# A change of buffer layout, of one scaling's engine and of six relu blocks' places at the seams of a two-layer graph kernel

## The chip, the cores and the metric

The kernel runs on one core of one Trainium2 chip, in float32 throughout. The metric is the device time of one execution in microseconds (us). The kernel before the change takes 2812.73 us, the median of three runs (2812.05 to 2813.75). Its profile is of one execution of 2812.97 us, whose recorded span is 2811.2 us.

A core has five engines with a queue each, which work through their own instructions in the order in which they were written down and wait for each other through semaphores: TensorE (PE; PEld is its loading of weights), VectorE (DVE), ScalarE (ACT), GpSimd (POOL) and SyncE (SP), which only starts transfers here. Matmuls write to PSUM; all other data lie in SBUF.

## The reference

There are 128 graphs of 64 tokens with 768 features. The input is normalised per token and cut at zero; two layers of attention over the given adjacency follow, and the input is added at the end:

```python
for l in range(2):
    m_left = einsum('bsh,oh->bso', h, W_left[l])
    m_right = einsum('bsh,oh->bso', h, W_right[l])
    u_left = einsum('bih,bjh->bij', h, m_left) / sqrt(768)
    u_right = einsum('bih,bjh->bij', h, m_right) / sqrt(768)
    u = u_left * adj_tri + u_left * diag_mask + u_right * swapaxes(adj_tri, 1, 2)
    e = exp(u) * adj
    attention = e / (sum(e, axis=2) + 1e-10)
    h_lin = einsum('bsh,oh->bso', h, W_lin[l]) + b_lin[l]
    ctx = matmul(attention, h_lin)
    h = relu(layer_norm(ctx, ln_a[l], ln_b[l]))
return x + h
```

## The kernel before, in words

**Passes.** The work is done in four passes, one after the other: `pass_one(0)`, `pass_two(0)`, `pass_one(1)`, `pass_two(1)` (L683 to L686). A pass goes over 16 blocks `u` of 512 tokens. Pass one of a layer projects a block with the left and the right weights (`project`, L344) and makes the attention from it (`scores`, L370, with a chain of small steps called softmax); the attention goes to DRAM. Pass two makes `h_lin` (`linear`, L607), multiplies the attention with it (`context`, L541) and normalises (`finish`, L566). In layer 0 the normalised rows `z` go to DRAM, four stores for each pair of row blocks (L594); the first pass of layer 1 loads them again as `x` (`load_rows`, L226, L243), transposes them on DVE to `xb` (L314), stores these (L310), loads them back feature by feature as `ht` (L248) and applies relu with `ln_a` and `ln_b` on ACT (`affine`, L250, L255), six instructions of 128x512 for a block.

**Matrix products.** A 768 by 768 product is done in 15 products of thirds of the features, with sums of weights and of tokens made ahead (a fast matrix multiplication). `ORDER` (L109) gives them: step 0 goes to PSUM bank X, 1 to Z, 2 to X, 3 to Y, and so on. The sums of tokens `ts` are made on POOL (L144; eleven for a block, 13 buffers). `read` (L182) brings a bank into the outputs, `m` in pass one and `hl` in pass two: the first product of an output is copied by ACT (L189), the others are added by DVE (L144). A bank is not written again before it has been read: step 2 stands still until ACT has read X of step 0.

**Order.** Nothing is scheduled by a tool. Each step runs two numbered slots (`run(base + 2 * i)` after its first half and `run(base + 2 * i + 1)` after its reads), and `put` and `put_all(slot, fs, step)` enter what else is to be issued in each slot, on whichever engine. So a slot settles the place of an instruction among the others of its engine. In the last block of pass two the two halves of the rows are done one after the other (L661, L663), 30 slots each, and the first block of the next layer is made ready beside them: `load_h(1, 1, 0)`, the six relu instructions from slot 22 and the sums of tokens from slot 30 (L658 to L660).

**End of the pass.** After the last half, `finish(u, 1)` (L666) runs the last context and normalisation: two squares on ACT (L577) with their sums, a square root (L579), the inverse on DVE (L582, L583), and for each of two row blocks a scaling (`scaled`, L585; on ACT in layer 0, L592) and its two stores.

**Buffers.** Each pass opens a pool of its own, and the pool of the next pass takes the same bytes of SBUF. Inside a pool the names get their places in the order in which they are first asked for. The pools are opened with `reuse_waits="tile"`: the first write of a tile waits for the last use of those old tiles that lay on its bytes, and for no others. By the built program, in KB from the start of the pool (`hl` is two buffers, `at` three, `x` and `adj` two, `z` three):

| pool | places before the change |
|---|---|
| pass one, layer 0 | `x` 0-12, `adj` 12-16, `xb` 16-28, `m` 28-52, `wm` 52-54 |
| pass two, layer 0 | `at` 0-3, `hl` 3-27, `z` 27-36, `x` 36-48, `xb` 48-60 |
| pass one, layer 1 | `adj` 0-4, `x` 4-16, `xb` 16-28, `m` 28-52, `wm` 52-54 |
| pass two, layer 1 | `a`, `b` 0-6, `at` 6-9, `hl` 9-33, `z` 33-45, `xr` 45-57 |

`wm` and `adj` are worked on by the softmax of the last block until the end of pass one (L396 to L414), after PE has gone on to pass two.

Of the kernel before, what the change touches and what calls it, by code (L numbers as in the profile page):

```python
# [10 lines left out]
F32 = mybir.dt.float32  # L11
I32 = mybir.dt.int32
AF = mybir.ActivationFunctionType
# [4 lines left out]
def kernel(  # L18
# [24 lines left out]
    nc = tc.nc  # L43
    B, S, H = x.shape
    L = w_lin.shape[0]
    P = 128
    C = H // P
# [4 lines left out]
    Q = 4  # L52
    T = Q * P
    TH = T // 2
    NB = B * S // T
# [203 lines left out]
    def transpose_rows(l, u, pool):  # L259
# [57 lines left out]
        todo.append(store)  # L317
        return todo


    def pass_one(l, aside):
        with tc.tile_pool(name=f"one{l}", bufs=2, reuse_waits="tile") as sp:
            ADJ, CHAIN, M = {}, {}, {}

            def load_adj(u):
                ADJ[u] = sp.tile([P, Q, 2, S], F32, name="adj")
# [200 lines left out]
    def pass_two(l, aside):  # L527
        last = l == L - 1
        with tc.tile_pool(name=f"two{l}", bufs=2, reuse_waits="tile") as sp:
            if last:  # L530
                for name, src in (("a", ln_a), ("b", ln_b)):
                    row(name, src[l], 0, H, sp.tile([P, H], F32, name=name, bufs=1))
            AT, HL = {}, {}

            def load(u):
                if (2, l, u) not in HT:
                    load_h(2, l, u)
                AT[u] = sp.tile([P, Q, S], F32, name="at", bufs=3)
                nc.sync.dma_start(AT[u], ATT[l][u])

            def context(u, r):  # L541


                hl, at = HL[u], AT[u]
                lo, hi = slice(0, S), slice(S, P)
                cx = [ps_aux.tile([P, 2, T], F32, name="aux") for _ in range(2)]
                for n in range(2):
                    for (j, k, i) in ((lo, 0, lo), (hi, 0, hi), (lo, 1, hi), (hi, 1, lo)):
                        q = r + 2 * k
                        m = n if j == lo else 1 - n  # L550
                        nc.tensor.matmul(cx[k][i, m, :HH], at[j, q, :], hl[j, q, m * HH:(m + 1) * HH],  # L551
                                         start=True, stop=True)
                return [c[:, :, :HH] for c in cx]

            def batch(r, k, h):
                return 4 * (h if k == 0 else 1 - h) + r + 2 * k

            XS = {}

            def residual(u, r):  # L560
                XS[u, r] = [sp.tile([P, H], F32, name="xr", bufs=4) for _ in range(2)]
                for k in range(2):
                    for h in range(PAIR):
                        nc.sync.dma_start(XS[u, r][k][h * S:(h + 1) * S], x[u * NBB + batch(r, k, h)])

            def finish(u, r):  # L566

                cx = context(u, r)
                zs = [sp.tile([P, H], F32, name="z", bufs=4 if last else 3) for _ in range(2)]
                if last and not u and not r:  # L570
                    residual(u, r)
                two = "p (n d) -> p n d"
                ss = stat.tile([P, 2], F32, name="ss")
                sd = stat.tile([P, 2], F32, name="sd1")
                rs = stat.tile([P, 2], F32, name="rs1")
                for k in range(2):
                    nc.scalar.activation(zs[k].rearrange(two, n=2), cx[k], AF.Square, accum_out=ss[:, k:k + 1])  # L577

                nc.scalar.activation(sd, ss, AF.Sqrt, bias=floor, scale=1.0 / (H - 1.0))  # L579

                def inverse():
                    nc.vector.tensor_scalar_add(rs, sd, EPS_LN)  # L582
                    nc.vector.reciprocal(rs, rs)  # L583

                def scaled(k):  # L585
                    if last:
                        nc.vector.scalar_tensor_tensor(  # L587
                            zs[k].rearrange(two, n=2), cx[k], rs[:, k:k + 1],
                            rows["a"].rearrange(two, n=2), op0=ALU.mult, op1=ALU.mult)
                        nc.gpsimd.tensor_add(zs[k], zs[k], rows["b"])  # L590
                        return
                    nc.scalar.activation(zs[k].rearrange(two, n=2), cx[k], AF.Copy, scale=rs[:, k:k + 1])  # L592
                    for h in range(PAIR):
                        nc.sync.dma_start(ROWS[u][batch(r, k, h)], zs[k][h * S:(h + 1) * S])  # L594

                def done(k):
                    if last:
                        xs = XS[u, r]
                        nc.vector.scalar_tensor_tensor(xs[k], zs[k], 0.0, xs[k], op0=ALU.max, op1=ALU.add)
                        for h in range(PAIR):  # L600
                            nc.sync.dma_start(out[u * NBB + batch(r, k, h)], xs[k][h * S:(h + 1) * S])
                        if k and (u < NB - 1 or r == 0):
                            residual(u + r, 1 - r)

                return [inverse] + [lambda k=k: scaled(k) for k in range(2)] + [lambda k=k: done(k) for k in range(2)]

            def linear(u, rs, base, ends, more):  # L607

                b, w = tokens_of((2, l, u)), W[l, "n"]
                if rs[0] == 0:  # L610
                    HL[u] = sp.tile([P, Q, H], F32, name="hl", bufs=2)
                hl, seen = HL[u], set()
                bank = {"X": AHEAD.pop()}
                early = {0: 3, 2: 5, 6: 9}
                for i, (s, at, t, _) in enumerate(ORDER):
                    if i in FIRST and i not in PRELOAD:
                        bank[at] = fresh(l, i, rs)
                    p = bank[at]
                    for n, r in enumerate(rs):
                        for c in range(K2):  # L620
                            nc.tensor.matmul(p[:, n], b[t][:, c, r * P:(r + 1) * P], w[s][:, c, :],  # L621
                                             start=(i in FIRST and i not in PRELOAD and n == c == 0),
                                             stop=(c == K2 - 1), skip_group_check=True)
                        if n == 0:
                            run(base + 2 * i)
                    read(p, lambda o: hl[:, o % 2 * 2 + rs[0]:o % 2 * 2 + rs[0] + len(rs), o // 2 * D:(o // 2 + 1) * D],
                         i, seen)
                    if i in early:
                        bank[FIRST[early[i]][0]] = fresh(l, early[i], rs)
                    if i == 11 and more:  # L630
                        AHEAD.append(fresh(l, 0, more))
                    if i in ends:
                        what, slots = ends[i]
                        for f, n in zip(finish(*what), slots):
                            put(n, f)
                    run(base + 2 * i + 1)

            load(0)
            for u in range(NB):
                turn = not last and u >= NB - 2  # L640
                if u + 1 < NB:
                    load(u + 1)
                    put_all(9 if u else 15, affine(2, l, u + 1))
                    put_sums_t((2, l, u + 1), 15 if u else 21, 1, 0)
                    if turn:
                        load_rows(1, 0, sp)
                        put_all(10, transpose_rows(1, 0, sp), 2)
                    if u in aside:
                        aside[u]()
                    ends = {}  # L650
                    if u:
                        ends = {0: ((u - 1, 0), (6, 7, 8, 11, 12)), 7: ((u - 1, 1), (20, 21, 22, 30, 30))}
                    linear(u, (0, 1), 0, ends, (0, 1) if u + 2 < NB else (0,))
                    for n in sorted(plan):
                        plan[n - 30] = plan.pop(n)
                else:
                    if turn:
                        load_h(1, 1, 0)  # L658
                        put_all(22, affine(1, 1, 0))
                        put_sums_t((1, 1, 0), 30, 2, 30)  # L660
                    linear(u, (0,), 0, {0: ((u - 1, 0), (12, 13, 15, 19, 21)),  # L661
                                        11: ((u - 1, 1), (34, 35, 36, 42, 44))}, (1,))
                    linear(u, (1,), 30, {4: ((u, 0), (50, 51, 52, 56, 58))}, ())  # L663
                    for n in sorted(plan):
                        run(n)
                    for f in finish(u, 1):  # L666
                        f()
# [48 lines left out]
```

## Time and profile before

| what | us |
|---|---|
| time, median of three | 2812.73 |
| span of the profiled execution | 2811.2 |
| pass one, layer 0, with the start | 0 to 936 |
| pass two, layer 0 | 936 to 1412 |
| pass one, layer 1 | 1412 to 2323 |
| pass two, layer 1 | 2323 to 2811 |
| step of 8 matmuls at full pace | 1.73 |
| step of 4 matmuls (last block of pass two, by halves) | 0.86 |

The ends of the passes are where the timeline shows the first matmul of the next one. A line of the timeline or of the groups names the source line, the engine, the operation, what it writes and reads, and in square brackets how long its engine stood idle ahead of it and what ended that. A line of the waits gives who waited for whom, then the sum in us, the number of times, and the longest.

### The profile page before, as it was taken

What the parts mean: (1) busy time and instruction counts of PE and PEld (TensorE: products, weight loads), DVE (VectorE), ACT (ScalarE), POOL (GpSimd) and SP (SyncE); (2) the same over time, 40 slices, a digit from 0 to 9 for tenths busy, and PEclk for the clock granted to TensorE, in tenths of its full rate; (3) what the DMA queues carried; (4) which work ended last, traced back from release to release, by engine and by line L of the source; (5) the groups of instructions that cost most, each with busy time, mean ns of one, the idle gap of its engine ahead of it and who ended that gap; (6) DMA issues with size and microseconds to landing.
All of it is one profiled execution on the core that took longest, in us unless ns stands there. A gap on an engine that the chain in (4) does not pass through costs nothing.

```text
span 2811.2 us, 46104 instructions
## 1 busy us (share of the span) xinstructions
PE 2755.9 (98%) x18712; PEld 2343.6 (83%) x18712; DVE 1338.1 (48%) x2222; ACT 838.0 (30%) x1453; POOL 1189.7 (42%) x935
## 2 busy tenths in 40 slices
PE   7999999999999999999999999999999999999997
PEld 6888888888888888888778888888888888888885
DVE  6455554454444332322334434443444335666666
ACT  2122222322231244444422121112111214545443
POOL 3343333223323455565423343223322335887875
PEclk9999999999999999999999999999999999999999
DMA  5632443234322243333563432343234304555654
GB/s 156 165 76 74 100 116 78 74 96 120 79 73 76 98 159 110 99 125 105 148 159 84 119 92 74 83 117 94 74 80 118 75 25 145 159 170 160 184 161 124
DMA packets 234068, 310.80 MB, mean 111 GB/s; under 512 B 54144, under 2 KB 184448, under 8 KB 225664
## 3 DMA queue, kind: packets, MB, share of 16 engines
q1 hardware_dynamic: 233568, 307.06, 39.9%
q8 instruction: 149, 2.44, 0.4%
q10 hardware_dynamic: 288, 0.79, 0.1%
q14 instruction: 63, 0.52, 0.1%
HBM read 202.91 MB, written 104.86 MB: 109 GB/s over the span
## 4 chain that ended last, share of the span: by engine, by line
PE 94%; DVE 2%; issue 1%; DMA 1%; POOL 1%; ACT 1%; SPq 0%; DVEq 0%; ACTq 0%; POOLq 0%
PE X L356 23%; PE V L356 15%; PE X L621 12%; PE Y L356 11%; PE Z L356 8%; PE V L621 8%; PE Y L621 6%; PE aux L382 5%; PE Z L621 4%; PE aux L551 3%; POOL w_r L144 1%; DVE m L144 0%; DMA z<-z 0%; DVE wm L396 0%; DMA x<-in_x_dram 0%
## 5 line engine op out<-in xcount | busy, mean ns | idle before, releaser
L144 POOL TENSOR_TENSOR ts<-ht 128x512 f32<-128x512 f32 x441 | 585.5, 1339 | 1249.1 <-DMA ht<-h 560.8
L189 ACT ACTIVATE m<-X 128x512 f32<-128x512 f32 x256 | 152.3, 595 | 1117.8 <-PE X L356 585.9
L144 POOL TENSOR_TENSOR ts<-ht,ts 128x512 f32<-128x512 f32 x189 | 248.8, 1324 | 155.4 <-PE X L621 78.2
L144 DVE TENSOR_TENSOR m<-m,V 128x512 f32<-128x512 f32 x256 | 174.2, 681 | 272.0 <-PE V L356 272.0
L144 DVE TENSOR_TENSOR m<-m,X 128x512 f32<-128x512 f32 x256 | 163.8, 681 | 252.0 <-PE X L356 251.4
L356 PE MATMUL X<-ts,w_l 128*128 128x256 f32 x1024 | 246.6, 384 | 10.7 <-ACT m L189 5.1
L621 PE MATMUL X<-w_n,ts 128*128 128x256 f32 x1024 | 245.1, 381 | 6.0 <-ACT hl L189 5.7
L356 PE MATMUL X<-ts,w_r 128*128 128x256 f32 x1024 | 241.9, 379 | 0.0
L144 DVE TENSOR_TENSOR m<-m,Z 128x512 f32<-128x512 f32 x128 | 88.0, 688 | 322.7 <-ACT m L189 254.4
L356 PEld LDWEIGHTS X<-ts,w_l 128*128 128x128 f32 x1024 | 194.1, 192 | 43.0 <-issue 6.0
L621 PEld LDWEIGHTS X<-w_n,ts 128*128 128x128 f32 x1024 | 192.0, 190 | 37.6 <-ACT hl L189 6.3
L356 PEld LDWEIGHTS X<-ts,w_r 128*128 128x128 f32 x1024 | 192.3, 190 | 28.7
L255 ACT ACTIVATE ht<-ht,b_col,a_col 128x512 f32<-128x512 f32 x192 | 143.1, 804 | 149.2 <-DMA ht<-h 149.2
L621 PE MATMUL Y<-w_n,ts 128*128 128x256 f32 x768 | 182.9, 380 | 0.0
L356 PE MATMUL Y<-ts,w_l 128*128 128x256 f32 x768 | 181.8, 380 | 0.0
L356 PE MATMUL Y<-ts,w_r 128*128 128x256 f32 x768 | 181.4, 379 | 0.0
L189 ACT ACTIVATE hl<-X 128x512 f32<-128x512 f32 (+1 forms) x136 | 77.7, 571 | 332.8 <-PE X L621 323.2
L621 PEld LDWEIGHTS Y<-w_n,ts 128*128 128x128 f32 x768 | 146.5, 191 | 20.1
L356 PEld LDWEIGHTS Y<-ts,w_l 128*128 128x128 f32 x768 | 146.4, 191 | 20.1
L356 PEld LDWEIGHTS Y<-ts,w_r 128*128 128x128 f32 x768 | 145.9, 190 | 19.8
L590 POOL TENSOR_TENSOR z<-z,b 128x768 f32<-128x768 f32 x64 | 115.4, 1814 | 95.4 <-DVE z L587 95.4
L144 DVE TENSOR_TENSOR hl<-hl,X 128x512 f32<-128x512 f32 (+1 forms) x136 | 83.2, 653 | 146.2 <-PE X L621 144.3
(105 smaller groups left out, 4680.7 us busy)
## 6 DMA issues: line engine op xcount, KB each, us to landing
ht<-h SPq DMA_DIRECT2D x63, 1536.0 KB, 7.2
h<-xb SPq DMA_DIRECT2D x124, 384.0 KB, 6.5
z<-z SPq DMA_DIRECT2D x128, 192.0 KB, 2.8
x<-z SPq DMA_DIRECT2D x128, 192.0 KB, 8.6
xr<-in_x_dram SPq DMA_DIRECT2D x128, 192.0 KB, 3.8
out_dram<-xr SPq DMA_DIRECT2D x128, 192.0 KB, 2.6
x<-in_x_dram SPq DMA_DIRECT2D x120, 192.0 KB, 8.5
adj<-in_adj_dram SPq DMA_DIRECT2D x64, 128.0 KB, 2.7
```

The source lines that it names most:

```text
L144: (eng.tensor_add if sign == "+" else eng.tensor_sub)(o, a, b)
L189: nc.scalar.activation(to(o), p, AF.Copy, scale=1.0 if sign == "+" else -1.0)
L255: nc.scalar.activation(ht, ht, AF.Relu, bias=cols[1][:, c:c + 1], scale=cols[0][:, c:c + 1])
L356: nc.tensor.matmul(p[:, g], w[ORDER[i][0]][:, c, g * P:(g + 1) * P], b()[t][:, c, :], start=(new and g == c == 0), stop=(c == K2 - 1), ski ...
L382: nc.tensor.matmul(p[h * S + e:h * S + e + 32, q, e:e + 96], ht[:, c, b * S + e:b * S + e + 32], mb[:, e:e + 96], start=(c == 0), stop=(c ...
L551: nc.tensor.matmul(cx[k][i, m, :HH], at[j, q, :], hl[j, q, m * HH:(m + 1) * HH], start=True, stop=True)
L590: nc.gpsimd.tensor_add(zs[k], zs[k], rows["b"])
L621: nc.tensor.matmul(p[:, n], b[t][:, c, r * P:(r + 1) * P], w[s][:, c, :], start=(i in FIRST and i not in PRELOAD and n == c == 0), stop=(c ...
```

## The change

It has three parts.

- **Layout.** A new helper `places` asks once for a tile of each name at the start of a pool, in a chosen order, and does nothing with it; with that the names' places are settled. In pass one of layer 0 the order becomes `x`, `xb`, `m`, `adj`, `wm`; in pass two of layer 0 `hl`, `at`, `x`, `xb`, `z`; in pass one of layer 1 `m`, `adj`, `x`, `xb`, `wm`. Pass two of layer 1 is left as it is. The aim is that a tile which is written first in a pass lies on tiles that the pass ahead has long been done with.
- **The last scaling on two engines.** In the last block's last `finish` of layer 0 the second of the two scalings goes to DVE.
- **The first relu blocks of the next layer spread.** The six instructions of L255 for the first block of layer 1 go to slots 28, 31, 34, 37, 40, 43 instead of 22 to 27, and the first five sums of tokens to slots 38 to 46 instead of 30 to 38. The other six sums stay at slots 51 to 57.

By the built program the places become:

| pool | places after the change |
|---|---|
| pass one, layer 0 | `x` 0-12, `xb` 12-24, `m` 24-48, `adj` 48-52, `wm` 52-54 |
| pass two, layer 0 | `hl` 0-24, `at` 24-27, `x` 27-39, `xb` 39-51, `z` 51-60 |
| pass one, layer 1 | `m` 0-24, `adj` 24-28, `x` 28-40, `xb` 40-52, `wm` 52-54 |
| pass two, layer 1 | as before |

No instruction of PE, POOL or SP is added, removed or moved among the others of its engine; ACT loses one scaling, which DVE gets, and the six L255 change places on ACT.

```diff
+    def places(pool, shapes, names):
+        for n in names:
+            shape, bufs = shapes[n]
+            pool.tile(shape, F32, name=n, bufs=bufs)
...
     def pass_one(l, aside):
...
+            shapes = {"x": ([P, 2, H], 2), "xb": ([P, H // 32, Q, 32], 1), "m": ([P, C, NBB, 2, S], 1),
+                      "adj": ([P, Q, 2, S], 2), "wm": ([P, Q, 2, S], 1)}
+            places(sp, shapes, ("m", "adj", "x", "xb", "wm") if l else ("x", "xb", "m", "adj", "wm"))
...
     def pass_two(l, aside):
...
+            else:
+                places(sp, {"hl": ([P, Q, H], 2), "at": ([P, Q, S], 3), "x": ([P, 2, H], 2),
+                            "xb": ([P, H // 32, Q, 32], 1), "z": ([P, H], 3)}, ("hl", "at", "x", "xb", "z"))
...
-                    nc.scalar.activation(zs[k].rearrange(two, n=2), cx[k], AF.Copy, scale=rs[:, k:k + 1])
+                    if (u, r, k) == (NB - 1, 1, 1):
+                        nc.vector.tensor_scalar_mul(zs[k].rearrange(two, n=2), cx[k], rs[:, k:k + 1])
+                    else:
+                        nc.scalar.activation(zs[k].rearrange(two, n=2), cx[k], AF.Copy, scale=rs[:, k:k + 1])
...
                         load_h(1, 1, 0)
-                        put_all(22, affine(1, 1, 0))
-                        put_sums_t((1, 1, 0), 30, 2, 30)
+                        put_all(28, affine(1, 1, 0), 3)
+                        put_sums_t((1, 1, 0), 38, 2, 30)
```

## The prediction, made before the changed kernel was run

> **What bounds the kernel now.** I read the page's part 1 first, then the chain of waits through the whole span, then the waits of PE alone, and then the timeline of the places where PE stood.
>
> ```profile
> PE 2755.9 (98%) x18712; PEld 2343.6 (83%) x18712; DVE 1338.1 (48%) x2222; ACT 838.0 (30%) x1453; POOL 1189.7 (42%) x935
> ```
>
> PE sets the time: it is idle for only 55.3 us of 2811.2. No instruction of PE changes, so the change can only win back places where PE stands or is slowed. By the windows view 35.1 of them lie in the first 85 us (19.8: loads, first normalisation) and after 2780 us (15.2), which no part of the change touches. Outside these, the two largest holes are changes of pass: 7.9 us at 1376 to 1430 and 2.7 at 930 to 950. The chain of waits at the seam between pass two of layer 0 and pass one of layer 1:
>
> ```profile
> 1391.41 3.52 ACT ht L255 x5
> 1394.93 0.28 ACT hl L189
> ...
> 1395.25 2.07 PE X L621 x4
> 1397.32 1.36 PE Y L621 x4
> ...
> 1410.41 2.03 PE aux L551 x16
> ...
> 1414.36 0.91 ACT z L592
> ...
> 1417.06 3.24 DMA z<-z
> ...
> 1420.40 0.60 ACT m L189
> ...
> 1421.14 3.75 PE X L356 x8
> 1424.90 2.09 PE Y L356 x8
> 1426.99 1.73 PE X L356 x8
> ```
>
> Start and duration in us. Two stalls are seen, each followed by slow matmuls. At 1391.41 five relu blocks of the next pass (L255) stand on ACT ahead of the read of bank X that PE needs. At 1417.06 the first write of `m` waits until a store of `z` has landed. The same from the side of PE, over the whole span:
>
> ```profile
> PE X L621 <- ACT hl L189: 5.7, 3, 2.8
> PE X L356 <- ACT m L189: 5.1, 1, 5.1
> ```
>
> The first row's 5.7 us are 2.75 at 1392.5, 2.70 at the seam between pass one and two of layer 0, and 0.30 at the same seam of layer 1. The timeline of those last two:
>
> ```profile
> 941.39 0.45 DVE L414 STREAM_TRANSPOSE wm<-adj 128x256 f32<-128x256 f32 x1
> ...
> 941.96 0.60 ACT L189 ACTIVATE hl<-X 128x512 f32<-128x512 f32 x1 [2.38 <-DVE wm L414]
> ...
> 942.61 1.99 PE L621 MATMUL X<-w_n,ts 128*128 128x256 f32 x8 [2.70 <-ACT hl L189]
> ```
>
> ```profile
> 2326.41 0.42 ACT L402 ACTIVATE adj<-adj 128x256 f32<-128x256 f32 x1 [12.04 <-DVE adj L400]
> 2326.73 0.58 ACT L189 ACTIVATE hl<-X 128x512 f32<-128x512 f32 x1
> ...
> 2327.46 1.96 PE L621 MATMUL X<-w_n,ts 128*128 128x256 f32 x8 [0.30 <-ACT hl L189]
> ```
>
> In layer 0 `hl` waits for the last reader of `adj`, whose bytes it takes; in layer 1 it lies elsewhere and follows the exponential at once.
>
> The windows view shows the granted clock (the last but two figure) around the two stalls of the other seam:
>
> ```profile
> 1390.00:1404.00 14.00, 11.25 (x53) 8.42 (x52) 2.30 (x7) 10.98 (x25) 8.27 (x7) 0.88 0.21 58
> 1416.00:1426.00 10.00, 4.94 (x14) 3.95 (x14) 0.69 (x1) 1.73 (x4) 0.00 (x0) 0.66 0.93 229
> ```
>
> At half speed for 14 x 0.12 x 2 = 3.4 us and 10 x 0.34 x 2 = 6.8 us.
>
> **What the Trainium skill says.** "TensorE: Matmul & The Clock Gate", What's actually happening: the array runs at half clock after an idle window of about 3.4 us, in free-running windows. The trace agrees on the size (3.4 and 6.8 us); 2.75 us of idleness were enough at 1392.5, 2.70 at 942 were not, so where the gap falls decides. "VectorE: DVE Perf Modes", Why PSUM operands drop a tier: fp32 from PSUM runs at the base rate; in "PSUM — Partial Sum Buffer", Specifications, ScalarE and VectorE read PSUM in parallel if not in the same bank. The trace agrees with both: L587 on DVE, of the added operation's shape, takes 1010 ns; at 1407.07 DVE adds from X while ACT scales from aux (L592, 1406.62 to 1408.31).
>
> **The change part by part.**
>
> *Layout, pass one to two of layer 0.* In before, counted in KB from the pool's start, `hl` took 3-27 where `x` (0-12) and `adj` (12-16) had been. Now `x`, `xb` lie at 0-24, and `hl` takes 0-24; `x` was last read at 846.8 and the stores of `xb` were issued by then to 852, over 80 us earlier. The read then follows the exponential as in layer 1: stall 0.30 instead of 2.70, **2.4 us saved**. The new waits this makes (`at` over `m`, done at 936.2; `z` over `adj` and `wm`, whose stores are issued from 941.9 to 947.7, while the first write of `z` starts at 968.5) end long before they are asked for: nothing.
>
> *Layout, pass two of layer 0 to pass one of layer 1.* `m` lay at 28-52, on `z` (27-36), so its first write waited for the last stores. Now `m` takes 0-24, exactly the two `hl`, whose last readers are the aux matmuls; these end at 1412.4, ahead of the X step that `m` copies. That wait is free.
>
> *One of the last two scalings on DVE.* ACT did two L592 (1.69 us from 1414.36), then the copy. Now it does one, 0.90, while DVE does the other from the same release. Cost on DVE 1.01 by L587 (0.80 to 1.0 as bounds: 768 elements at the 1.04 ns of the PSUM page's Specifications, an estimate, or the row with two inputs; I take the row). Behind it on DVE stands the add of bank Z, which needs ACT's copy of Z, 1416.7 at the earliest; DVE is free at about 1415.5. So nothing. The store on the queue is not delayed, its third issue was at 1416.46 anyway.
>
> Together: the ACT copy of X runs 1415.26 to 1415.86 instead of 1420.40 to 1421.00, and PE's third step may start near 1415.95. On pace it would start at 1412.36 + 2 x 1.73 + 0.1 fill = 1415.92. So the stall goes (5.06) and the half clock with it. On pace the fifth step comes at 1419.54; it came at 1426.99: **7.4 us saved**.
>
> *Relu blocks spread.* Six L255, slots 22 to 27, become slots 28, 31, 34, 37, 40, 43. They now stand singly between the reads that PE needs. Replay of ACT by its own durations (L255 0.72 back to back, reads and bias copies 0.28, squares 0.75, scalings 0.85): squares of the former block 1388.0 and, after the store that lands at 1389.1, 1389.1 to 1389.9; first relu 1390.2; read of X at 1391.67, as soon as PE has it, so X at 1392.34 has no stall. Bias, relu, read of Z, relu to 1394.0; read of X to 1394.3, next X at 1394.4 (0.3 late). Two scalings to 1396.25, which release the aux buffers of the context matmuls: these wait about 0.9. Relu, read to 1397.3. Squares of the next block: the second needs a `z` buffer whose store follows the scaling at 1395.4 by 3.4 (as at 1398.84 to 1402.2 before): 1398.8 to 1399.6. Then sqrt, relu, and only then the read for the ninth step (X), which starts at 1400.95 instead of 1403.82. On pace it would be at 1390.61 + 8 x 0.863 + 1.65 = 1399.2, so of 4.65 us lost about 1.8 stay: **2.9 us saved**, with 0 (each relu as exposed as before) and 4.6 (none) as ends.
>
> *First token sums on POOL* come eight slots later and wait for the fourth and sixth relu: first at 1397.0, the fourth at 1402, the last by 1412.1. In the new timing PE's first step of the pass is at 1409.5 and the step that needs the last one 14 steps later. Slack of over 10 us: nothing.
>
> Sum: 2.4 + 7.4 + 2.9 = 12.7; 2812.73 - 12.7 = 2800.0.
>
> **The rivals.** (a) *The rows for the next block hold DVE.* PE's unit is now 7.4 us nearer to its loads. L243's first four issue at 1419.2 to 1420.7, the last lands 5.8 us later, 1426.5. The DVE transposes that wait for them stand ahead of the bank X adds that the eleventh step (1429.76) needs: two transposes 1.83 and adds 1.28 give 1429.6. It just fits. If landing slips by 3 us, or a half-clock window is added, some 4.4 go: 2804.4. For it: the margin is 0.1 us. Against: that DMA is bound by SP's issues, which do not move. (b) *The relu blocks cost as much when spread*: ACT is busy 10.98 of 14 us there, for it; against, 4.7 of 10 us in the next stretch. Gives 2812.7 - 9.8 = 2802.9. (c) *All comes to pace*: 2.4 + 7.4 + 4.6, 2798.3. (d) *Slower*: nothing is won at 1390, and the loads land late enough (8 us of transfers doubled) to hold DVE for 8 us and start two half-clock windows (3.4 lost): -2.4 - 7.4 + 11.4, plus about 5 for token sums that then come late: 2819. Nothing in the profile speaks for it but that DMA is at 0.93 busy there.
>
> **How the numbers follow.** Main case 0.64 (2798.5 to 2801.5), (a) 0.12, (b) 0.10, (c) 0.10, (d) 0.04. The range 2797.0 to 2806.0 takes in the main case, (b), (c) and most of (a), widened for the store landings that I could only copy from before. The bound of 0.2% is 2807.1 downwards and 2818.4 upwards: faster 0.92, same 0.05 (a bad form of (a) with (b)), slower 0.03.
>
> **What would show it.** At 942 the PE stall on `hl` is about 0.3. PE has no wait on ACT `m` L189 and no half clock between 1385 and 1425 (by the old times). L255 stands singly, with stalls of PE on `hl` or aux of under 1 us each. L314 waits for `x<-z` about 2.5 us in the first unit of layer 1, and PE does not wait on `m` reads of DVE behind it. PE's wait of 0.30 at 2327 stays. Wrong would be: a new wait of the `m` write on anything, or the eleventh step standing on DVE for more than 1 us.

## The result and the profile after

The changed kernel takes 2800.0 us (median of 4 runs, 2796.77 to 2804.74), the kernel before beside it on the same chip 2812.39 (4 runs, 2810.76 to 2813.75). The ratio is 0.9958, with a 95% interval of 0.994 to 0.9975: faster by 0.25 to 0.6%. The prediction was 2800.0, in a range of 2797 to 2806. That the medians meet so exactly is partly luck: the three terms of the sum were 12.7 us and came out as 11.9, and single runs of one kernel differ by several microseconds. So the terms are judged one by one, in the trace.

Part 1 of the page, after:

```profile
PE 2755.9 (98%) x18712; PEld 2342.4 (84%) x18712; DVE 1340.9 (48%) x2223; ACT 838.7 (30%) x1452; POOL 1190.1 (42%) x935
```

PE is busy for as long as before. Its idle time fell from 55.3 to 2803.0 - 2755.9 = 47.1 us, the 8.2 us by which the profiled spans differ. PE's waits over the whole span, the same two rows as in the prediction (sum, times, longest, all in us):

```profile
PE X L637 <- ACT hl L189: 1.1, 3, 0.5
...
PE X L366 <- ACT m L189: 0.7, 2, 0.5
```

They were 5.7 and 5.1. The two stalls of 2.7 on `hl` and the one of 5.1 on `m` are gone; what is left is about half a microsecond at any one place. (The lines have moved with the edit: L621 is now L637, L356 is L366, L577 is L590, L579 is L592, L582 is L595, L592 is L608 on ACT and L606 on DVE; in single runs they lie a few lines off these.)

The chain of waits at the seam between the layers, after (start, duration, piece):

```profile
1393.63 0.70 ACT ht L255
...
1396.21 2.76 DMA z<-z
...
1411.51 0.89 DVE rs L595
...
1412.63 0.90 ACT z L608
1413.53 0.50 ACT m L189
1414.16 1.97 PE X L366 x8
```

Relu blocks (L255) are single pieces now. A store of `z` still stands in the chain, but at 1396, ahead of a square of the half block before, and no longer ahead of the copy of `m`, which follows the scaling directly. One piece has grown: the 0.89 us of DVE at 1411.51, for a tile of 128 by 2 numbers, were 0.18 in the chain of the kernel before. The run rs1 is about it.

The windows view (stretch, length, then busy time of PE, PEld, DVE, ACT and POOL, granted clock, DMA share, GB/s), after:

```profile
1390.00:1400.00 10.00, 9.86 (x50) 6.81 (x50) 2.35 (x7) 8.88 (x19) 2.65 (x3) 1.00 0.30 80
1410.00:1420.00 10.00, 9.47 (x43) 8.06 (x44) 3.44 (x5) 4.31 (x10) 2.37 (x2) 1.00 0.50 138
```

The clock is full in both, where it had been 0.88 and 0.66 around the two stalls.

**Three stretches.** To compare traces in which the same work starts at different times, I measure from a first matmul to a first matmul. A goes from the scores of the last block of pass one, layer 0, to the fourth step of pass two. B1 is the second half of the last block of pass two, layer 0: first step to last context. B2 goes from the first step of pass one, layer 1, to its fifth step. All are in us, each from one trace. A ratio is to runs of the kernel before beside it on the same chip; their medians lay between 2812.4 and 2813.8.

| kernel | A | B1 | B2 | start to A | median (range, runs) | ratio to before (95%) |
|---|---|---|---|---|---|---|
| before | 12.65 | 19.74 | 14.47 | 931.79 | 2812.39 | |
| changed | 10.20 | 17.00 | 7.78 | 934.52 | 2800.0 (2796.77-2804.74, 4) | 0.9958 (0.994-0.9975) |
| layout | 10.66 | 20.04 | 7.85 | 931.61 | 2802.16 (2800.7-2803.83, 5) | 0.9962 (0.9948-0.9976) |
| spread | 14.74 | 16.99 | 14.63 | 931.66 | 2810.45 (2807.48-2812.31, 12) | 0.9992 (0.9983-1.0) |
| nosplit | 10.49 | 16.98 | 8.54 | 931.69 | 2800.89 (2799.57-2801.96, 4) | 0.9957 (0.9942-0.9972) |
| mold | 10.20 | 16.98 | 14.49 | 934.70 | 2805.82 (2804.03-2810.26, 12) | 0.9978 (0.997-0.9987) |
| adjfirst | 12.63 | 17.01 | 7.76 | 933.49 | 2803.96 (2800.17-2806.01, 7) | 0.9967 (0.9956-0.9978) |
| oldone0 | 10.09 | 16.98 | 7.76 | 930.66 | 2800.01 (2799.93-2800.96, 3) | 0.9957 (0.9941-0.9973) |
| early | 10.20 | 17.00 | 7.76 | 934.22 | 2804.55 (2800.14-2806.22, 8) | 0.9969 (0.9959-0.9979) |
| rs1 | 10.21 | 16.99 | 7.11 | 930.26 | 2799.45 (2796.32-2801.87, 4) | 0.9955 (0.9938-0.9972) |
| better | 10.12 | 16.31 | 7.11 | 933.21 | 2798.69 (2795.72-2801.67, 5) | 0.9945 (0.9932-0.9957) |
| after2 (changed, again) | 10.39 | 16.98 | 7.76 | 932.39 | 2801.54 (2799.55-2803.1, 5) | 0.9955 (0.9942-0.9969) |

B1 and B2 repeat to a few hundredths wherever the code in them is alike, and A to about half a microsecond, in part since in some traces a short pause that the profile puts down to issue falls into it. So they tell apart what the medians can't. The change won 12.65 - 10.20 = 2.45 in A, 19.74 - 17.00 = 2.74 in B1 and 14.47 - 7.78 = 6.69 in B2, 11.88 together. The medians differ by 12.4. The profiled spans differ by only 8.2, because the trace of the changed kernel lost 2.73 before A began (934.52 against 931.79) and a net 0.9 after B2, in small pieces both ways. The 2.73 isn't the change's doing: nosplit has the very same code up to A and comes there at 931.69, rs1 at 930.26. It is taken up in the last section.

### The profile page after: what moved, and what is told of

The parts are those of the page before. It is cut to its first block, busy times and chain, and to the rows that moved or that the text cites. A ratio compares the mean times of both kernels' runs of the same rounds, so it can differ in the third digit from the quotient of the medians.

```text
span 2803.0 us, 46102 instructions
## 1 busy us (share of the span) xinstructions
PE 2755.9 (98%) x18712; PEld 2342.4 (84%) x18712; DVE 1340.9 (48%) x2223; ACT 838.7 (30%) x1452; POOL 1190.1 (42%) x935
## 4 chain that ended last, share of the span: by engine, by line
PE 94%; DVE 2%; DMA 1%; ACT 1%; issue 1%; SPq 0%; POOL 0%; DVEq 0%; ACTq 0%; POOLq 0%
PE X L366 23%; PE V L366 15%; PE X L637 12%; PE Y L366 11%; PE Z L366 8%; PE V L637 8%; PE Y L637 6%; PE aux L392 5%; PE Z L637 4%; PE aux L564 3%; DVE m L144 1%; DMA ht<-h 0%; DMA h<-xb 0%; ACT ht L255 0%; DVE w_l L144 0%
## 5 line engine op out<-in xcount | busy, mean ns | idle before, releaser
L366 PE MATMUL X<-ts,w_l 128*128 128x256 f32 x1024 | 246.6, 384 | 6.0 <-DVE w_l L144 2.1
L637 PE MATMUL X<-w_n,ts 128*128 128x256 f32 x1024 | 244.2, 380 | 0.9 <-ACT hl L189 0.6
L366 PE MATMUL X<-ts,w_r 128*128 128x256 f32 x1024 | 242.1, 379 | 0.2 <-ACT m L189 0.2
L366 PEld LDWEIGHTS X<-ts,w_l 128*128 128x128 f32 x1024 | 194.2, 192 | 38.5 <-DVE m L144 4.6
L637 PEld LDWEIGHTS X<-w_n,ts 128*128 128x128 f32 x1024 | 191.6, 190 | 32.2 <-DVE hl L144 2.3
L366 PEld LDWEIGHTS X<-ts,w_r 128*128 128x128 f32 x1024 | 192.2, 190 | 29.6 <-ACT m L189 0.6
L255 ACT ACTIVATE ht<-ht,b_col,a_col 128x512 f32<-128x512 f32 x192 | 144.1, 808 | 142.9 <-DMA ht<-h 142.9
L637 PE MATMUL Y<-w_n,ts 128*128 128x256 f32 x768 | 182.4, 379 | 0.0
L366 PE MATMUL Y<-ts,w_l 128*128 128x256 f32 x768 | 181.8, 380 | 0.0
L366 PE MATMUL Y<-ts,w_r 128*128 128x256 f32 x768 | 181.4, 379 | 0.0
L366 PEld LDWEIGHTS Y<-ts,w_l 128*128 128x128 f32 x768 | 146.4, 191 | 20.0
L637 PEld LDWEIGHTS Y<-w_n,ts 128*128 128x128 f32 x768 | 145.9, 190 | 19.8
L366 PEld LDWEIGHTS Y<-ts,w_r 128*128 128x128 f32 x768 | 145.9, 190 | 19.8
```

The source lines that it names most:

```text
L255: nc.scalar.activation(ht, ht, AF.Relu, bias=cols[1][:, c:c + 1], scale=cols[0][:, c:c + 1])
L366: nc.tensor.matmul(p[:, g], w[ORDER[i][0]][:, c, g * P:(g + 1) * P], b()[t][:, c, :], start=(new and g == c == 0), stop=(c == K2 - 1), ski ...
```

## The experiments

Each is the changed kernel with one thing undone, added or moved, unless it says otherwise.

### The layout alone (layout), and the rest alone (spread)

layout keeps the new places and undoes the other two parts:

```diff
-                    if (u, r, k) == (NB - 1, 1, 1):
-                        nc.vector.tensor_scalar_mul(zs[k].rearrange(two, n=2), cx[k], rs[:, k:k + 1])
-                    else:
-                        nc.scalar.activation(zs[k].rearrange(two, n=2), cx[k], AF.Copy, scale=rs[:, k:k + 1])
+                    nc.scalar.activation(zs[k].rearrange(two, n=2), cx[k], AF.Copy, scale=rs[:, k:k + 1])
...
-                        put_all(28, affine(1, 1, 0), 3)
-                        put_sums_t((1, 1, 0), 38, 2, 30)
+                        put_all(22, affine(1, 1, 0))
+                        put_sums_t((1, 1, 0), 30, 2, 30)
```

> The three new orders of buffers alone, both last scalings on ACT and the relu blocks at slots 22 to 27 as before. Three stretches are read from the trace. A: from the first matmul of the scores of the last block of pass one, layer 0, to the first of the fourth step (bank Y) of pass two; before 12.65 us, changed kernel 10.20. B1: from the first step of the second half of the last block of pass two, layer 0, to its last context; 19.74 and 17.01. B2: from the first step of pass one, layer 1, to its fifth (bank X); 14.47 and 7.78. My theory, that the layout removes the two waits, the split only one scaling, and that a DVE instruction waiting for POOL costs the changed kernel 0.7 us of B2 because the sums of tokens come later there: A 10.2, B1 19.7, B2 7.0 on pace plus 0.85 for the second scaling on ACT = 7.9, time 2803.4. Rival, that the split is what frees the copy of m: B2 stays over 12, time about 2810. Rival, that the 0.7 us have another cause than POOL: B2 8.6.

spread is the kernel before with the new slots alone:

```diff
-                        put_all(22, affine(1, 1, 0))
-                        put_sums_t((1, 1, 0), 30, 2, 30)
+                        put_all(28, affine(1, 1, 0), 3)
+                        put_sums_t((1, 1, 0), 38, 2, 30)
```

> The relu blocks and sums of tokens spread as in the change, buffers and scalings as before. My theory: A 12.65, B1 17.0; B2 14.5, or 15.2 if the DVE instruction waits 0.7 for POOL here too and so the last store of z goes out later; time 2812.4 - 2.7 to - 2.0 = 2809.7 to 2810.4. Rival, that spreading gains nothing of its own: B1 19.7, time 2812.4.

Measured: layout wins A (10.66; 0.40 of it is a pause of PE that the profile puts down to issue, inside the scores) and B2 (7.85), and leaves B1 as it was (20.04). spread wins B1 (16.99) and nothing in B2 (14.63). So B1 belongs to the spread relu blocks, A and B2 to the layout. What spread does not win is the same DMA wait as before. The timeline of spread at the seam (start, duration, engine, line, operation; in brackets how long the engine stood and for what):

```profile
1420.39 0.60 ACT L189 ACTIVATE m<-X 128x512 f32<-128x512 f32 x1 [4.38 <-DMA z<-z]
```

PE's stall on `m` is longer here than before, 5.78 against 5.06: the small DVE addition ahead of the stores took 0.86 us instead of 0.17, as the expectation allowed for. That B2 is still near 14.5 is chance: of the window of half clock, 6.8 us in both traces, 3.5 fell into the stall here and 2.4 in before, so it cost less after it.

In time layout comes to 0.9962 and spread to 0.9992. spread won 2.75 in B1, but its A is 2.1 longer than that of before, though the stall on `hl` there is the same 2.70: 0.42 of it is a pause put down to issue, and the rest came with half clock, which in that run followed the stall. The code up to A is that of before, so this is not the spreading's doing.

### The scaling not split (nosplit)

```diff
-                    if (u, r, k) == (NB - 1, 1, 1):
-                        nc.vector.tensor_scalar_mul(zs[k].rearrange(two, n=2), cx[k], rs[:, k:k + 1])
-                    else:
-                        nc.scalar.activation(zs[k].rearrange(two, n=2), cx[k], AF.Copy, scale=rs[:, k:k + 1])
+                    nc.scalar.activation(zs[k].rearrange(two, n=2), cx[k], AF.Copy, scale=rs[:, k:k + 1])
```

> The changed kernel with both last scalings on ACT. My theory: A 10.2, B1 17.0, B2 7.78 + 0.85 = 8.6, PE's wait on the copy of m about 1.4 instead of 0.53; time 2800.9. Rival, that the split matters more since a second scaling on ACT also delays the stores: B2 over 10. Rival, that DVE's scaling itself costs as much as it saves: B2 7.8.

B2 is 8.54 instead of 7.78, so the split is worth 0.76, near the 0.8 by which ACT's part gets shorter (1.69 to 0.90). PE waits 1.29 for the copy of `m` here and 0.53 in the changed kernel:

```profile
1412.35 1.96 PE L366 MATMUL X<-ts,w_l 128*128 128x256 f32 x8 [1.29 <-ACT m L189]
```

The medians (2800.89 and 2800.0) can't tell this apart; the stretch can.

nosplit is also layout with the spread added, and nothing else. B2 is 8.54 here and 7.85 there: so the spreading, which wins 2.7 in B1, costs 0.69 in B2. In the changed kernel the split just about pays for that. The cause of this cost is found further down (rs1).

### `m` back on `z` (mold)

Only the layout of the seam between the layers is undone; split and spreading stay.

```diff
-            places(sp, shapes, ("m", "adj", "x", "xb", "wm") if l else ("x", "xb", "m", "adj", "wm"))
+            places(sp, shapes, ("adj", "x", "xb", "m", "wm") if l else ("x", "xb", "m", "adj", "wm"))
...
-            else:
-                places(sp, {"hl": ([P, Q, H], 2), "at": ([P, Q, S], 3), "x": ([P, 2, H], 2),
-                            "xb": ([P, H // 32, Q, 32], 1), "z": ([P, H], 3)}, ("hl", "at", "x", "xb", "z"))
```

> The changed kernel with only pass one, layer 0, in the new order of buffers; pass two, layer 0, and pass one, layer 1, lie as before, so that m again takes the bytes of z, while split and spread stay. My theory: A 10.2 (hl lies on x, xb and m, all read by then), B1 17.0, B2 14.5 to 15.2, since the copy of m waits for the stores of z; time 2807 to 2808. Rival, that split and spread are enough: B2 7.8, time 2800.

B2 is 14.49, as in before. The timeline of mold at PE's third step of the pass:

```profile
1419.59 3.41 PE L366 MATMUL X<-ts,w_l 128*128 128x256 f32 x8 [5.79 <-ACT m L189]
```

PE stands 5.79 us although the scaling is split and the relu blocks are spread, and half clock follows (3.41 us for eight matmuls). With `m` on `z` the store alone sets when `m` can be written; all that the split brings is hidden behind it. The stall is 0.7 longer than in before, for the same reason as in spread, and the half clock costs that much less; that the sums meet is chance. mold runs at 0.9978, so that by the medians the layout of this seam is worth 5.8 us of the changed kernel's 12, by B2 all of the 6.7 there.

### The order of pass one, layer 0 (adjfirst, oldone0)

adjfirst puts `adj` at the start, so that `hl` has to lie on it again:

```diff
-            places(sp, shapes, ("m", "adj", "x", "xb", "wm") if l else ("x", "xb", "m", "adj", "wm"))
+            places(sp, shapes, ("m", "adj", "x", "xb", "wm") if l else ("adj", "x", "xb", "m", "wm"))
```

> The changed kernel, but in pass one, layer 0, adj takes the first 4 KB of the pool, so that the first hl of pass two lies on it again. My theory: the read of bank X waits for the last reader of adj again, A 12.65 instead of 10.20, or some 2 more if a half-clock window falls there as in the run with the spread alone (14.74); B1 17.0 and B2 7.8 as in the changed kernel. Rival, that A was gained by something else in the layout: A 10.2.

oldone0 gives pass one of layer 0 the order of the kernel before, `x` then `adj`, and keeps the new order of pass two:

```diff
-            places(sp, shapes, ("m", "adj", "x", "xb", "wm") if l else ("x", "xb", "m", "adj", "wm"))
+            places(sp, shapes, ("m", "adj", "x", "xb", "wm") if l else ("x", "adj", "xb", "m", "wm"))
```

> The changed kernel with pass one, layer 0, in its old order, x at 0-12 and adj at 12-16 KB, and pass two in the new one. By the built program the first hl takes 0-12 here, so it lies on x alone. My theory: A 10.2, so the reorder of pass one, layer 0, does nothing and that of pass two alone saves the 2.4 us. Rival: the second hl, on adj at 12-16, makes a wait: A 12.65, or a stall of PE one block later.

The timeline of the changed kernel at this seam, and then that of adjfirst:

```profile
941.87 0.42 ACT L412 ACTIVATE adj<-adj 128x256 f32<-128x256 f32 x1 [12.11 <-DVE adj L410]
942.20 0.58 ACT L189 ACTIVATE hl<-X 128x512 f32<-128x512 f32 x1
...
942.92 1.97 PE L637 MATMUL X<-w_n,ts 128*128 128x256 f32 x8 [0.30 <-ACT hl L189]
```

```profile
943.64 0.60 ACT L189 ACTIVATE hl<-X 128x512 f32<-128x512 f32 x1 [2.38 <-DVE wm L424]
...
944.29 1.99 PE L637 MATMUL X<-w_n,ts 128*128 128x256 f32 x8 [2.70 <-ACT hl L189]
```

adjfirst brings back the wait of 2.38 on the last reader of `adj` and PE's 2.70, to the hundredth: the overlap is the cause. But oldone0 is as good as the changed kernel (A 10.09). With pass two's `hl` asked for first, the first `hl` takes bytes 0 to 12 KB, which is `x` in the old order as well; the second `hl` lies partly on `adj`, but PE's only wait up to 1000 us is 0.3. mold, above, is the other half of this: there pass two has its old order and pass one the new one, and A is 10.20. So either of the two new orders wins A alone, and only one of them was needed.

### The rows for the next block earlier (early)

The rival given the largest chance was a DVE that stands on the rows being loaded. early puts all that prepares the second block of pass one, layer 1, the transposes among it, four slots ahead:

```diff
-                    slot = 14
+                    slot = 10 if l else 14
```

> The changed kernel with all of what prepares the second block of pass one, layer 1, four slots earlier (two matmul steps, 3.5 us), so that DVE comes to the transposes before the rows have landed. It tests the prediction's case (a). My theory, that a DVE held by landing rows holds PE only beyond a small margin: the four transposes end up ahead of the X adds of the ninth step, which then end about 1 us after the eleventh step should start; PE waits on DVE m 0.5 to 1.5 us there. Rival, that these waits never reach PE: no such wait. Other rival, that they reach it in full: over 3 us.

In the changed kernel the rows cost PE nothing, as its timeline shows:

```profile
1424.43 1.84 DVE L314 STREAM_TRANSPOSE xb<-x 128x768 f32<-128x768 f32 x2 [2.40 <-DMA x<-z]
...
1426.59 1.28 DVE L144 TENSOR_TENSOR m<-m,X 128x512 f32<-128x512 f32 x2 [0.33 <-PE X L366]
```

DVE waits 2.40 for the rows and then still has to wait for PE's X (0.33). Its adds end at 1427.87, 0.18 before the eleventh step starts (1428.05). In early:

```profile
1427.26 1.84 DVE L314 STREAM_TRANSPOSE xb<-x 128x768 f32<-128x768 f32 x2 [0.65 <-DMA x<-z]
...
1430.32 1.99 PE L366 MATMUL X<-ts,w_l 128*128 128x256 f32 x8 [2.42 <-DVE m L144]
```

PE stands for 2.42 us. I had expected 0.5 to 1.5; DVE stood on a second landing too (0.65 until 1427.26), and the adds came behind both. From the first step of the pass to the scores of its first block it took 57.17 us instead of 54.49, 2.7 longer. The queue of instructions behind a DMA wait on DVE is thus a real cost, and the changed kernel lies just on the right side of it.

### The scale factors without POOL in the way (rs1)

In B2 the changed kernel missed the forecast by 0.7 us. The timeline shows where: the addition to the two standard deviations (L595) takes 0.88 us, and it ends at 1412.39, 0.02 after a sum on POOL. The changed kernel first, then layout, whose sums are eight slots earlier:

```profile
1409.86 2.51 POOL L144 TENSOR_TENSOR ts<-ht 128x512 f32<-128x512 f32 x2
...
1411.51 0.88 DVE L595 TENSOR_SCALAR rs<-sd 128x2 f32<-128x2 f32 x1 [3.08 <-ACT sd L592]
...
1414.16 1.97 PE L366 MATMUL X<-ts,w_l 128*128 128x256 f32 x8 [0.53 <-ACT m L189]
```

```profile
1412.09 0.17 DVE L595 TENSOR_SCALAR rs<-sd 128x2 f32<-128x2 f32 x1 [3.08 <-ACT sd L592]
```

The Trainium skill ("SBUF — State Buffer", Who interferes with whom) says that DVE and GpSimd (POOL) share one pair of ports, that `tensor_scalar` can take it in a two-port mode, and that whoever is later is blocked until the other ends. This is what the line looks like. Its page "VectorE: DVE Perf Modes" (Side-by-side: where the cycles go for N=2048 bf16, the table) ties that mode to an outermost dimension, other than one, that is even or equal in source and destination. A single column has no such dimension. So the same arithmetic by single columns ought not to wait, whatever POOL does:

```diff
-                    nc.vector.tensor_scalar_add(rs, sd, EPS_LN)
+                    if not last and (u, r) == (NB - 1, 1):
+                        for k in range(2):
+                            nc.vector.tensor_scalar_add(rs[:, k:k + 1], sd[:, k:k + 1], EPS_LN)
+                    else:
+                        nc.vector.tensor_scalar_add(rs, sd, EPS_LN)
```

> The changed kernel, with the addition of the constant to the deviations in the very last normalisation of layer 0 done as two DVE instructions of 128x1 instead of one of 128x2. In the changed kernel the one took 0.88 us instead of 0.16 and ended 0.02 us after a sum of tokens on POOL. My theory, that an instruction of two columns takes the ports that POOL shares, and one of one column can't be split over them: two of 0.16, B2 7.78 - 0.72 + 0.2 = 7.2. Rival, that any DVE instruction in SBUF waits for POOL: first of them up to 0.9, B2 7.8 or more.

The timeline of rs1:

```profile
1405.61 2.49 POOL L144 TENSOR_TENSOR ts<-ht 128x512 f32<-128x512 f32 x2
...
1407.24 0.22 DVE L597 TENSOR_SCALAR rs<-sd 128x1 f32<-128x1 f32 x2 [3.08 <-ACT sd L592]
...
1409.22 1.97 PE L366 MATMUL X<-ts,w_l 128*128 128x256 f32 x8
```

Both columns together take 0.22 while POOL is in the middle of its sums: the first starts 0.41 into a sum, as the addition did in the changed kernel, and ends 0.70 before that sum does. PE's wait on `m` is gone from the line. B2 is 7.11. The forecast of 7.4 saved means 14.47 - 7.4 = 7.07: nearly the whole shortfall was this one instruction. It is also what the spreading cost in nosplit: with the sums eight slots later, one of them runs beside the addition.

### A further version (better), beside the changed kernel again (after2)

better takes rs1, gives the second scaling of the finish ahead to DVE as well, and moves the fifth relu block from slot 40 to 38:

```diff
-                    if (u, r, k) == (NB - 1, 1, 1):
+                    if (u, r, k) in ((NB - 2, 1, 1), (NB - 1, 1, 1)):
...
-                        put_all(28, affine(1, 1, 0), 3)
+                        for n, f in zip((28, 31, 34, 37, 38, 43), affine(1, 1, 0)):
+                            put(n, f)
```

> The changed kernel with the two DVE instructions of one column; besides, the fifth relu block at slot 38 instead of 40 (ahead of the read of the fifth step instead of behind the squares that follow it), and the second scaling of the half block before the last on DVE too. My theory, that the 1.9 us still lost in B1 are ACT's, 0.65 from the two scalings in a row that hold the context's banks and 0.7 to 0.9 from the relu block ahead of the ninth step's read: B1 15.5 to 15.8 instead of 17.0, B2 7.1, time about 2 us below the changed kernel's, 2798. Rival, that the ninth step waits for the store of z that the square needs, whatever stands behind it: B1 16.3 or more, time 2799.

> The changed kernel once more on the same chip, for the comparison. A 10.2, B1 17.0, B2 7.8, time 2800. From the runs so far the start up to the scores of the last block of pass one differs by up to 4 us from run to run, with the half-clock windows near 90 us: 930.3 to 931.8 without one or with a short one, 933.5 to 934.7 with one of 6.8 us. Theory, that this and not the change makes the spread: it falls into one of these groups again, and B1, B2 and A stay within 0.3 of their values.

B1 is 16.31, 0.69 less than in the changed kernel (17.00). I had hoped for 15.5 to 15.8; the rival of 16.3 or more was right. The timeline of better:

```profile
1394.32 1.55 PE L564 MATMUL aux<-hl,at 64*64 64x384 f32 x16
...
1397.69 0.81 ACT L590 ACTIVATE z<-aux 128x768 f32<-128x768 f32 x1 [0.91 <-DMA z<-z]
...
1399.24 1.13 PE L641 MATMUL X<-w_n,ht 128*128 128x256 f32 x4 [0.59 <-ACT hl L189]
```

The context matmuls take 1.55 where they took 2.30 in the changed kernel, so the second scaling on DVE did its part, but most of that time is only waited later. ACT stands on the store of an earlier `z` before it may write its second square, which starts 8.19 us after the first step of B1 in better and in the changed kernel alike. The ninth step waits for the read that ACT does after that; what moved it is that the relu block of 0.7 no longer stands between. A further buffer of `z` or an earlier store might help there; neither was tried. Together with 0.67 in B2, better saves 1.36 us by the stretches. The medians on the same chip are 2798.69 and 2801.54, the ranges overlap. It is the best version that I found, by the trace; the runs alone don't prove it.

## Why the prediction was right, point by point

- **2.4 at the seam of the passes of layer 0: 2.45.** The mechanism held (adjfirst). It was credited to the two new orders together, and either suffices (oldone0, mold). That no new wait would come of it was right too.
- **7.4 at the seam of the layers: 6.69.** The wait of `m` on a store of `z` is gone and nothing took its place (layout, mold). The split was worth 0.76. Its cost on DVE was 1.02 us, as the row with two inputs had it (1.01); the 0.80 from the page's rate per element, which stands there for writes of 2-byte elements, was too low. It was hidden, as forecast: DVE still waited 0.78 for its next add. The step that failed reads "Slack of over 10 us: nothing", on the first token sums of POOL that come eight slots later. It asked only who waits for the sums. It did not ask what is held up while they run: DVE's small addition, by the skill's account because both engines need the same ports. This cost 0.88 - 0.17 = 0.71 us of the path, and rs1 wins 0.67 of it back. With it fell the remark that PE would have no wait on the copy of `m`: 0.53 was left.
- **2.9 at the relu blocks: 2.74.** The replay of ACT by its own durations held: the second square, which waits for the store, started at 1399.08 and the ninth step at 1401.34, in a trace that is 0.28 later by then, so at 1398.80 and 1401.06 where 1398.8 and 1400.95 were worked out. The context matmuls took 2.30 us; those that wait for nothing take 1.52 (at 1386.75), so they waited about 0.8 where 0.9 was forecast. The 1.65 that the prediction counts as pace, from one start to the next, is what before took; without a wait it is 1.45. Rival (b), relu blocks as costly when spread, falls, and so does (c): by the prediction's count 1.9 of the 4.65 stayed lost (4.65 less 2.74). better won 0.69 of that; the rest lies mostly behind the store of `z`, as far as the traces show.
- **Rival (a), rows that hold DVE.** DVE's wait for the rows was 2.40, "about 2.5" in the prediction. The adds ended 0.18 before the step that needs them (0.1 was reckoned), and the rows could have come another 0.33 later without delaying the adds. But the sum was not right in its parts: it left out that the 2.9 won in B1 brings the eleventh step forward too, to 1428.05 instead of 1429.76, and that the loads would not stay where they were. SP issued the first of them at 1417.92 instead of 1419.20, and the rows were there at 1424.43 where 1426.5 was reckoned. The two errors nearly cancel, which is luck. early shows what lies on the other side of the margin.
- **Clock.** No half clock between 1376 and 1430, as forecast (granted clock 1.00 over that window, 0.91 in before). This was counted inside the two terms and came with them.
- **The sum.** 12.7 forecast, 11.88 found in the three stretches; about 0.7 of the gap is the addition behind POOL.

## What to carry to other kernels

A wait that comes from where a tile lies is worth looking for at every change of phase: find what lay on the bytes of the first tile written, and let it lie on what has been finished longest; to ask for the tiles once in the wanted order costs no instruction. When work on POOL is moved, ask not only who needs its result but which small DVE instructions on the path will then run beside it. And price a part by the stretch between two fixed instructions of the trace: medians could not have told 0.7 us here.

## What the hardware showed that I had not expected

**A tiny instruction on DVE can wait for a whole one on POOL.** Over the whole trace of the kernel before, the 64 additions `rs<-sd` of 128 by 2 take 0.15 to 0.17 us in the 22 cases in which POOL stood idle as they began, and 0.16 to 1.28 in the 42 in which it was busy. In 41 of these 42 the addition ended 0.02 to 0.03 us after the POOL instruction that was running. The reciprocals that follow them on the same tile (`rs<-rs`, also 128 by 2) never waited: 0.17 us in all 64, 26 of them begun beside a busy POOL. So it is not any small DVE instruction that waits. On the path the addition lost 0.71; as two single columns, beside a busy POOL, nothing of it (0.22 for both in rs1 and again in better). The runs fit the skill's account of the ports; that the shape alone turns the wait off was shown for this one size.

**The same pause is sometimes followed by half clock and sometimes not.** PE's stall at 942 was 2.70 us in before, adjfirst and spread; only in spread did a window of half clock (3.4 us at 943.1) follow, and A was 14.74 instead of about 12.65. Likewise in both kernels PE pauses near 89 us, 2.91 before and 3.10 after, put down to issue. In the trace of the changed kernel a window of 6.8 us at half clock begins at 91.2; the kernel before has none there. The four traces with such a window of 6.8 us that begins between 90.0 and 91.3 (changed, mold, adjfirst, early) reach A at 933.5 to 934.7, the others at 930.3 to 933.2. "TensorE: Matmul & The Clock Gate" (What's actually happening) tells of a window that runs freely, which agrees with this: where the pause falls in it is not the kernel's to choose. The page asks for an idle window of about 3.4 us; the traces show half clock after pauses of 2.70 and 2.75 already. These windows go with two or three microseconds of the scatter between traces, but not with all of it: before, with no such window up to A, comes there at 931.79, and rs1, with one of 3.4 us, at 930.26. What the pause at 89 itself comes from, and whether it can be closed, stays open; no run tried it.
